# One decoder layer on one core: rare paths under one branch, one item's row products moved, tokens of the last items turned earlier

## The chip, the cores and the metric

The kernel runs on one core of a Trainium2 chip. The metric is the device time of one execution in microseconds; the program is launched once and nothing is computed on the host. The five engines of the core are TensorE (PE in the profile, with its weight loads as PEld), VectorE (DVE), ScalarE (ACT), GpSimd (POOL) and SyncE (SP). Each works through its own queue in order, and they meet through semaphores. SP issues plain DMAs; POOL issues the indirect DMAs, which gather or scatter rows by a table of indices.

## What is computed

The reference is one decoder layer over 4 sequences of 512 tokens of width 256, all in float32: a selective scan, a gated linear attention over a context, and a mixture of 8 experts of which each token takes two. After each of the three stands a residual sum and a layer norm. Only the last one matters here:

```python
# x2: the 2048 tokens after the second norm; 8 experts, w1, w3: 256 x 1024, w2: 1024 x 256
top_vals, top_idx = top_k(x2 @ gate_w, 2)          # two experts for each token, with weights m1, m2
for e in the two experts of a token:
    y += m_e * (silu(x2 @ w1[e]) * (x2 @ w3[e])) @ w2[e]
out = layernorm(x2 + y)
```

Which token goes to which expert is known only on the chip. The first two parts use a fast form that holds as long as some values stay in bounds; otherwise an exact, slow form must be computed in their place.

## The kernel before

**Stages.** `layer1` does the scan, `attend_fast` the attention, both for all four sequences; `route` then finds for each sequence the two experts of every token, and `close` writes the normed rows to DRAM: to up to three copies `xd` from which tokens are gathered, and to `yd`, in which the sums are built. `tables` turns the routing into three tables of int32 (`tok`: row to gather, `wat`: where its weight lies, `dest`: row to add to). There are four versions v of the tables: v=0 when two sequences are routed, v=1 when three are, v=2 for all four, and v=3 for overflow blocks.

**Items.** The tokens of an expert are handled in blocks of 128. An item is one block (G=1) or two (G=2). For an item:

- `fetch` (L1512) gathers the rows on POOL;
- `turn` transposes them on TensorE into `pt` (L1582), and a VectorE copy (L1586) makes `xgT`;
- `up` multiplies by w1 and w3 (L1597, tile `pu`), ScalarE takes the silu (L1602, `si`), VectorE the product (L1603, `ht`); it yields after each PSUM tile, four times for G=1 and eight for G=2;
- `down` fetches the weights of the tokens (`weigh`, L1612), multiplies by w2 (`product`, L1619, tile `po`), scales on ScalarE (L1639, `y`) and adds the rows to `yd` by an indirect DMA (`scatter`, L1625).

These are the row products: those with w2.

**Order.** `work` goes over a list of items and keeps one item `pending`: in each step it turns and does `up` of item i, and only then `down` of item i-1, so that the `ht` of an item is ready when TensorE comes to its row products. The lists are `early` (experts 0 and 1, one block each, v=0), `mid` (experts 3 to 7, v=1), `late` (v=2, and five overflow blocks), and `final` (expert 2, four single blocks). `early` has a call of `work` of its own, during which the fourth sequence is still being finished: its norm, its routing and its tables are the generator `last`. After this call the last early item is sent through `down` at once, then what is left of `last` is issued, then a second call of `work` takes `mid` and `late`. In its second step `overflow` makes the tables v=3 and the number of overflow blocks `items`.

Statements set the order of one engine only in part. A scheduler lays the instructions into the queues by its own estimates, so that instructions of `last` stand among those of the items.

**Weights.** Each expert has 3 MB (w1, w3, w2, each one DMA on SP's queue, L1494). They go into a ring of three places; the DMA of a place waits until TensorE has read what lay there.

**End.** `finale` handles the four blocks of expert 2. In its first step it does the pending `down`, then loads all of `yd` into `x1` (L1707) for the last norm, and gathers the rows of its own four blocks from `yd`. Their products are added in SBUF (`settle`, L1763), normed and scattered straight into the output (`put`). The norm of all other rows (`norm_all`: statistics L1681 and L1682, scaling on VectorE L1694 and on ScalarE L1699) is spread between the items, as one long list on VectorE's queue; its rows are stored by SP (L1710).

**Rare paths.** Two things are decided at the end by a value that every engine loads into a register (L1822, `items`; L1855, `isure`), each with a branch of its own: `tc.If(n_items > NOV0)` (L1826) for more than five overflow blocks, and `tc.If(sure == 0)` (L1859) for the exact form of the whole layer, which has the first branch in it once more. With the inputs of this case neither is taken, so both are jumped over. At the end of each the queue holds waits for all its DMAs, on POOL also an instruction that sets the semaphores of its indirect DMAs (INC_SWDGE_SEM in the profile).

Of the kernel before, what the change touches and what calls it, by code (L numbers as in the profile page):

```python
# [1 line left out]

# [7 lines left out]
F32 = mybir.dt.float32  # L10
AF = mybir.ActivationFunctionType
ALU = mybir.AluOpType
# [30 lines left out]
def decoder_kernel(ctx: ExitStack, tc: tile.TileContext, t: dict, out: bass.AP):  # L43
# [61 lines left out]
    x1 = x1T = eT = wide = val = shed = None  # L105

# [843 lines left out]
    def attend_fast(ap, hrp, np_, pt, tri, onw, mix, part, gatew, close, rt, route):  # L950
# [4 lines left out]
        with ExitStack() as hs:  # L955
# [198 lines left out]
            nc.vector.tensor_tensor(isure, top, flag, ALU.mult)  # L1154
            return tails

    def layers23(fast):
# [3 lines left out]
        NF = FF // P  # L1161
        with ExitStack() as rest:
            mp = pool(rest, "l2", 1)

            dest, tok, wat = (
                [mp.tile([P, n], I32, tag=f"{s}{v}", name=f"{s}{v}")
                 for v, n in enumerate((P, P, P, NOV))]
                for s in ("dest", "tok", "wat")
            )
            eid = mp.tile([P, NOV], I32, tag="eid", name="eid")  # L1170
            items = mp.tile([1, 1], I32, tag="items", name="items")
# [21 lines left out]
            dr = rest.enter_context(tc.tile_pool(name="dr", bufs=1, space=DRAM))  # L1193

            xds = [
                dr.tile([(v + 2) * S, D], F32, tag=f"xd{v}", name=f"xd{v}") for v in range(3)
            ]
            wds = [
                dr.tile([(v + 2) * 2 * S, 1], F32, tag=f"wd{v}", name=f"wd{v}") for v in range(3)
            ]  # L1200
            yd = dr.tile([NT, D], F32, tag="yd", name="yd")
# [236 lines left out]
            def overflow():  # L1438
# [41 lines left out]
                nc.vector.tensor_copy(items, cum[0:1, NE - 1 : NE])  # L1480


            loads = 0

            def load_expert(e):

                nonlocal loads
                ew = ring[loads % 3]
                loads += 1
                w1 = ew.tile([P, 2, FF], F32, tag="w1", name="w1")  # L1490
                w3 = ew.tile([P, 2, FF], F32, tag="w3", name="w3")
                w2 = ew.tile([P, NF, D], F32, tag="w2", name="w2")
                for w, n in ((w1, "w1"), (w3, "w3"), (w2, "w2")):
                    nc.sync.dma_start(  # L1494
                        out=w, in_=t[n][bass.ds(e, 1)].rearrange("o (k p) f -> p (o k) f", p=P)
                    )
                return w1, w3, w2

            def weights_of(e):
                if isinstance(e, int):  # L1500
                    return load_expert(e)
                i = e[0]
                return load_expert(nc.values_load(
                    eid[0:1, i : i + 1], engines=[mybir.EngineType.SP], min_val=0, max_val=NE - 1,
                    skip_runtime_bounds_check_because="it is at most NE - 1 by its minimum",
                ))

            def fetch(v, cols):

                xg = xgp.tile([P, 2, D], F32, tag="xg", name="xg")  # L1510
                for g, c in enumerate(cols):
                    nc.gpsimd.indirect_dma_start(  # L1512
                        out=xg[:, g, :], out_offset=None, in_=xds[min(v, 2)][:, :],
                        in_offset=bass.IndirectOffsetOnAxis(ap=tok[v][:, c : c + 1], axis=0),
                    )
                return xg

            def own(e, *blocks):  # L1520
                return [e * NS + j for j in blocks]

            def static(v, e, *blocks):
                return v, own(e, *blocks)

            early = [(e, [static(0, e, 0)]) for e in range(NEARLY)]
            mid = [(e, [static(1, e, 0, 1)]) for e in range(NEARLY + 1, NE)]
            mid[-1][1].append(static(2, NE - 1, 2, 3))
            late = [(e, [static(2, e, 2, 3)]) for e in range(NE - 2, NEARLY, -1)]
            late += [(e, [static(2, e, 1, 2), static(2, e, 3)]) for e in range(NEARLY)]  # L1530
            late += [((i,), [(3, [i])]) for i in range(NOV0)]

            final = (NEARLY, [static(1, NEARLY, 0), static(1, NEARLY, 1)])
            final[1].extend([static(2, NEARLY, 2), static(2, NEARLY, 3)])
            rare = [((i,), [(3, [i])]) for i in range(NOV0, NOV)]

            weights = [load_expert(0), load_expert(1)]
# [29 lines left out]
            ring.append(right)  # L1567
# [8 lines left out]
            out_t = out.rearrange("b s d -> (b s) d")  # L1576

            def turn(xg, G):
                ps = pt.tile([P, 2, TS], F32, tag="pt", name="pt3")
                for g in range(G):  # L1580
                    for k in range(2):
                        nc.tensor.transpose(  # L1582
                            ps[:, k, g * P : (g + 1) * P], xg[:, g, k * P : (k + 1) * P], ident
                        )
                xT_ = xtp.tile([P, 2, TS], F32, tag="xgT", name="xgT")
                nc.vector.tensor_copy(xT_[:, :, : G * P], ps[:, :, : G * P])  # L1586
                return xT_

            def up(xT_, G, w1, w3, ht):

                N, U = G * P, TS // (G * P)
                for f in range(0, NF, U):
                    ps = pup.tile([P, 2, U, N], F32, tag="pu", name="pu")
                    for u in range(U):
                        for j, w in enumerate((w1, w3)):
                            for k in range(2):
                                nc.tensor.matmul(  # L1597
                                    ps[:, j, u, :], w[:, k, (f + u) * P : (f + u + 1) * P],
                                    xT_[:, k, :N], start=(k == 0), stop=(k == 1),
                                )  # L1600
                    si = sip.tile([P, U * N], F32, tag="si", name="si")
                    nc.scalar.activation(si, ps[:, 0].rearrange("p u n -> p (u n)"), AF.Silu)  # L1602
                    nc.vector.tensor_tensor(  # L1603
                        ht[:, f * N : (f + U) * N], ps[:, 1].rearrange("p u n -> p (u n)"), si, ALU.mult
                    )
                    yield

            def inner(G):
                return htp.tile([P, NF * G * P], F32, tag="ht", name="ht")

            def weigh(wg, v, c):
                nc.gpsimd.indirect_dma_start(  # L1612
                    out=wg, out_offset=None, in_=wds[min(v, 2)][:, :],
                    in_offset=bass.IndirectOffsetOnAxis(ap=wat[v][:, c : c + 1], axis=0),
                )

            def product(ps, g, G, ht, w2):
                for f in range(NF):
                    nc.tensor.matmul(  # L1619
                        ps, ht[:, (f * G + g) * P : (f * G + g + 1) * P], w2[:, f, :],  # L1620
                        start=(f == 0), stop=(f == NF - 1),
                    )

            def scatter(rows, v, c, src, **kw):
                return nc.gpsimd.indirect_dma_start(  # L1625
                    out=rows[:, :],
                    out_offset=bass.IndirectOffsetOnAxis(ap=dest[v][:, c : c + 1], axis=0),
                    in_=src, in_offset=None, bounds_check=NT - 1, oob_is_err=False, **kw,
                )

            def down(v, cols, ht, w2):
                ps = pop.tile([P, 2, D], F32, tag="po", name="po")
                y = yp.tile([P, 2, D], F32, tag="y", name="y")
                wg = xgp.tile([P, 2], F32, tag="wg", name="wg")
                for g, c in enumerate(cols):
                    weigh(wg[:, g : g + 1], v, c)
                for g, c in enumerate(cols):
                    product(ps[:, g, :], g, len(cols), ht, w2)
                    nc.scalar.activation(y[:, g, :], ps[:, g, :], AF.Copy, scale=wg[:, g : g + 1])  # L1639
                    scatter(yd, v, c, y[:, g, :], compute_op=ALU.add)  # L1640

            def work(visits, weights, ahead=(), between=None):

                after = [e for e, _ in (*visits, *ahead)][len(weights) :]
                line = [(n, v, cols) for n, (_, its) in enumerate(visits) for v, cols in its]
                xgs = [fetch(v, cols) for _, v, cols in line[:2]]
                pending = None
                for i, (n, v, cols) in enumerate(line):  # L1650
                    G = len(cols)
                    xT_ = turn(xgs.pop(0), G)
                    w1, w3, w2 = weights[n]
# [312 lines left out]
```

## Time and profile before

| | us |
|---|---|
| time, median of 3 runs (lowest to highest) | 719.35 (714.34 to 723.76) |
| time of the profiled execution | 718.58 |
| its span, first to last instruction | 716.7 |
| TensorE busy | 663.3 (93%) |
| TensorE weight loads busy | 502.6 (70%) |
| VectorE, ScalarE, GpSimd busy | 307.1, 240.2, 220.4 |
| mean granted TensorE clock | 0.958 of full speed |

Times in the profile count from the first instruction. An engine's busy time leaves out register, branch, semaphore and DMA-issuing instructions; these are found by their source line, with a q behind the engine's name (POOLq). In a timeline each row has start, length, engine, line, operation, tiles, a count, and in brackets how long the engine sat idle before it and what released it. One `product` or one matmul of `up` in the source makes two TensorE records.

### The profile page before, as it was taken

The page shows a single profiled execution, that of the slowest core. Times are in us where ns is not written, and L with a number is a line of the kernel's source. Part 1 is how long each engine was busy: PE and PEld are TensorE (multiplying, and loading weights), DVE is VectorE, ACT ScalarE, POOL GpSimd, SP SyncE. Part 2 cuts the span into 40 slices and gives each one's busy share as a digit, 9 for nine tenths or more (in the row PEclk, how much of TensorE's full clock was granted, in tenths as well). Part 3 has the DMA queues.
Part 4 walks back from the last instruction along what each step waited for, and adds up shares of the span by engine and source line. Part 5 has one row for each costly group of instructions (what it writes and reads, how often), then busy time and mean ns, then how long its engine had stood idle before and what let it go on. Part 6 is the DMA issues. An engine that isn't in the chain of part 4 may idle for free. (4 is left out here: it accounts for less than half of the span.)

```text
span 716.7 us, 9223 instructions
## 1 busy us (share of the span) xinstructions
PE 663.3 (93%) x3447; PEld 502.6 (70%) x3447; DVE 307.1 (43%) x788; ACT 240.2 (34%) x460; POOL 220.4 (31%) x248
## 2 busy tenths in 40 slices
PE   5979879998999899889999999999999999999991
PEld 2413356765633445778888888888888999999890
DVE  0796855669453787856222111211111121111640
ACT  2438760223366575443212111111111111211450
POOL 0412231000144557366033332233321412332210
PEclk9999998999988899799999999999999999999996
DMA  8200050110820305695546625345661624882620
GB/s 280 100 1 0 1 176 1 30 30 9 303 70 1 118 19 176 219 321 165 188 135 206 205 62 160 112 126 177 200 193 37 185 75 140 294 294 57 206 84 16
DMA packets 61119, 92.71 MB, mean 129 GB/s; under 512 B 8728, under 2 KB 47968, under 8 KB 60800
## 3 DMA queue, kind: packets, MB, share of 16 engines
q1 hardware_dynamic: 51872, 80.25, 32.7%
q0 software_dynamic: 8096, 9.60, 7.0%
q10 hardware_dynamic: 1088, 2.10, 0.8%
q8 instruction: 31, 0.51, 0.3%
q14 instruction: 32, 0.26, 0.1%
HBM read 78.78 MB, written 13.80 MB: 129 GB/s over the span
## 5 line engine op out<-in xcount | busy, mean ns | idle before, releaser
L1597 PE MATMUL pu<-xgT,w 128*128 128x128 f32 (+1 forms) x1600 | 266.6, 327 | 1.6 <-DVE xgT L1586 1.5
L1597 PEld LDWEIGHTS pu<-xgT,w 128*128 128x128 f32 x1600 | 243.2, 193 | 23.9 <-ACT si L1602 1.9
L1603 DVE TENSOR_TENSOR ht<-pu,si 128x256 f32<-128x256 f32 x148 | 62.6, 423 | 227.5 <-ACT si L1602 227.0
L1619 PE MATMUL po<-w,ht 128*128 128x256 f32 x592 | 136.4, 380 | 2.5 <-DVE ht L1603 2.5
L1602 ACT ACTIVATE si<-pu 128x256 f32<-128x256 f32 x148 | 56.7, 384 | 196.3 <-PE pu L1597 194.7
L1619 PEld LDWEIGHTS po<-w,ht 128*128 128x128 f32 x592 | 109.0, 190 | 17.6 <-DVE ht L1603 3.3
L1625 POOL DMA_INDIRECT yd<-y,dest x33 | 53.3, 1616 | 146.6 <-ACT y L1639 127.0
L202 PE MATMUL xz<-xT,win 128*128 128x512 f32 x128 | 59.9, 624 | 10.3 <-DMA win<-in_win 7.9
L1512 POOL DMA_INDIRECT xg<-xd,tok x37 | 36.9, 997 | 80.7 <-PE pt L1582 65.6
L202 PEld LDWEIGHTS xz<-xT,win 128*128 128x128 f32 x128 | 24.7, 197 | 43.9 <-issue 38.8
L981 POOL TENSOR_TENSOR ct<-ct,tri 128x128 f32<-128x128 f32 x64 | 32.7, 529 | 47.2 <-ACT ct L980 44.6
L1639 ACT ACTIVATE y<-po,wg 128x256 f32<-128x256 f32 x33 | 15.6, 474 | 92.5 <-PE po L1619 92.5
L418 PE MATMUL fpy<-mt,xs 128*128 128x512 f32 (+3 forms) x128 | 39.5, 462 | 0.9 <-DVE fsz L422 0.8
L221 DVE SCALAR_TENSOR_TENSOR acc<-xp,convw,acc 128x2048 f32<-128x2048 f32 x12 | 30.7, 2571 | 21.6 <-POOL acc L216 21.6
L980 ACT ACTIVATE ct<-pq,eT 128x512 f32<-128x512 f32 (+3 forms) x64 | 30.6, 523 | 22.9 <-PE pq L970 22.8
L970 PE MATMUL pq<-x1T,ctxT 64*128 64x512 f32 (+3 forms) x128 | 33.8, 501 | 3.3 <-ACT ct L980 3.2
L1612 POOL DMA_INDIRECT wg<-wd,wat x33 | 32.6, 989 | 9.9 <-issue 9.6
L418 PEld LDWEIGHTS fpy<-mt,xs 128*128 128x128 f32 x128 | 23.4, 202 | 13.6 <-issue 7.2
L988 PE MATMUL ph<-ct,val 128*64 128x512 f32 (+3 forms) x128 | 32.7, 495 | 0.0
L1586 DVE COPY xgT<-pt 128x256 f32<-128x256 f32 (+1 forms) x25 | 13.8, 551 | 41.6 <-PE pt L1582 41.6
L439 PE MATMUL fpo<-fwout,fsz 128*128 128x256 f32 x128 | 29.9, 394 | 0.0
L970 PEld LDWEIGHTS pq<-x1T,ctxT 64*128 64x128 f32 x128 | 13.7, 193 | 23.0 <-ACT ct L980 10.9
(263 smaller groups left out, 623.2 us busy)
## 6 DMA issues: line engine op xcount, KB each, us to landing
w<-in_w SPq DMA_DIRECT2D x57, 1024.0 KB
xd<-x SPq DMA_DIRECT2D x9, 512.0 KB
xT<-in_xT ACTq DMA_DIRECT2D x4, 512.0 KB
ctxT<-in_ctxT SPq DMA_DIRECT2D x1, 2048.0 KB
val<-in_ctx SPq DMA_DIRECT2D x4, 512.0 KB
fxr<-in_x SPq DMA_DIRECT2D x4, 512.0 KB
yd<-x SPq DMA_DIRECT2D x4, 512.0 KB
x<-yd SPq DMA_DIRECT2D x4, 512.0 KB
```

Source lines behind the costliest of these rows:

```text
L202: nc.tensor.matmul(ps, win[:, k, c * P : (c + 1) * P], xT[:, k, b * S : (b + 1) * S], start=(k == 0), stop=(k == 1),)
L418: nc.tensor.matmul(ps[:, j * P :], xs[j][:, c, :], mt[b][j], start=(j == 0), stop=(j == NB - 1),)
L970: nc.tensor.matmul(ps[:, :w], ctxT[rows, p, s0 : s0 + P], x1T[rows, p, s0 : (b + 1) * S], start=True, stop=True,)
L981: nc.gpsimd.tensor_tensor(ct[:, :P], ct[:, :P], tri, ALU.mult)
L988: nc.tensor.matmul(po[DH * e : DH * (e + 1), tb * P :], val[:, b * NB + tb, 2 * p + e, :], cts[e], start=(tb == 0), stop=(tb == NB - 1),)
L1512: nc.gpsimd.indirect_dma_start(out=xg[:, g, :], out_offset=None, in_=xds[min(v, 2)][:, :], in_offset=bass.IndirectOffsetOnAxis(ap=tok[v][: ...
L1597: nc.tensor.matmul(ps[:, j, u, :], w[:, k, (f + u) * P : (f + u + 1) * P], xT_[:, k, :N], start=(k == 0), stop=(k == 1),)
L1602: nc.scalar.activation(si, ps[:, 0].rearrange("p u n -> p (u n)"), AF.Silu)
L1603: nc.vector.tensor_tensor(ht[:, f * N : (f + U) * N], ps[:, 1].rearrange("p u n -> p (u n)"), si, ALU.mult)
L1612: nc.gpsimd.indirect_dma_start(out=wg, out_offset=None, in_=wds[min(v, 2)][:, :], in_offset=bass.IndirectOffsetOnAxis(ap=wat[v][:, c : c + ...
L1619: nc.tensor.matmul(ps, ht[:, (f * G + g) * P : (f * G + g + 1) * P], w2[:, f, :], start=(f == 0), stop=(f == NF - 1),)
L1625: return nc.gpsimd.indirect_dma_start(out=rows[:, :], out_offset=bass.IndirectOffsetOnAxis(ap=dest[v][:, c : c + 1], axis=0), in_=src, in_ ...
```

## The change

The diff does three things, and moves the expert code into functions of its own for it.

1. **One branch at the end.** `overflow` now forms one number, `items`: 0 when nothing rare is needed, 1 when only further overflow blocks are, 2 or more when the fast form does not hold. All engines load this one number, `finale` asks for it before the last `settle`, and `tc.If(case > 0)` holds both rare paths. So that the overflow path can stand outside the pools of the common path, the tables v=2 and v=3 are stored to DRAM (`tds`), and `many` loads them again; `tok`, `wat` and `dest` of a version become three parts of one tile `tab`. The rare path for overflow blocks now also does expert 2 once more.
2. **The last early item's row products** are no longer issued before the second call of `work` but are handed to it as `pending`: they come after the first `up` of `mid`.
3. **The tokens of the last items are turned sooner:** in `finale`, item i+1 is turned after the third of the four steps of item i's `up`, not before its own.

```diff
-            weights, pending = work(early, weights, mid)
-            down(*pending)
+            weights, pending = xp.work(xp.early, weights, xp.mid)
             for _ in last:
                 pass
-            weights, pending = work(
-                mid + late, weights, [final], lambda i: overflow() if i == 1 else None
+            weights, pending = xp.work(
+                xp.mid + xp.late, weights, [xp.final], lambda i: overflow() if i == 1 else None,
+                pending,
             )
-            ys, sent = finale(final, weights[0], pending)
-            n_items = nc.values_load(items, ...)
-            with tc.If(n_items > NOV0):
...
+            return xp.finale(xp.final, weights[0], pending)
...
-        layers23(True)
-    sure = nc.values_load(isure, ...)
-    with tc.If(sure == 0):
-        kept = ExitStack()
-        with kept:
-            activations(False)
-            layer1_steps()
-            layers23(False)
+        case = layers23(True)
+    with tc.If(case > 0):
+        with tc.If(case == 1):
+            many()
+        with tc.If(case > 1):
+            kept = ExitStack()
+            with kept:
+                activations(False)
+                layer1_steps()
+                n_items = layers23(False)
+            with tc.If(n_items > NOV0):
+                many()
```

In `work`:

```diff
-            def work(visits, weights, ahead=(), between=None):
+        def work(visits, weights, ahead=(), between=None, pending=None):
...
-                pending = None
                 for i, (n, v, cols) in enumerate(line):
```

In `finale`:

```diff
+            ahead = turn(xgs.pop(0), 1)
             for i, (v, (c,)) in enumerate(line):
-                xT_ = turn(xgs.pop(0), 1)
+                xT_ = ahead
                 hts.append(inner(1))
                 for q, _ in enumerate(up(xT_, 1, w1, w3, hts[-1])):
...
+                    if q == 2 and xgs:
+                        ahead = turn(xgs.pop(0), 1)
...
             product(ps[:, 0, :], 0, 1, hts[-1], w2)
+            case = nc.values_load(items, ...)
             settle(N - 1, ps[:, 0, :])
             scales(rows[N - 1], rows[N - 1] + 1)
             put(N - 1)
-            return ys, sent
+            return case
```

In `overflow` and `attend_fast`:

```diff
-            nc.vector.tensor_tensor(isure, top, flag, ALU.mult)
+            nc.vector.tensor_tensor(sure, top, flag, ALU.mult)
...
-                nc.vector.tensor_copy(items, cum[0:1, NE - 1 : NE])
+                for td, tb in zip(tds, tabs[2:]):
+                    nc.sync.dma_start(out=td, in_=tb)
+                if not fast:
+                    nc.vector.tensor_copy(items, cum[0:1, NE - 1 : NE])
+                    return
+                more = rt("more", [1, 1])
+                nc.vector.tensor_scalar(more, cum[0:1, NE - 1 : NE], NOV0 + 0.5, None, ALU.is_gt)
+                nc.vector.scalar_tensor_tensor(more, sure, -2.0, more, ALU.mult, ALU.add)
+                nc.vector.tensor_scalar(items, more, 2.0, None, ALU.add)
```

The order in which the built program lays this into the queues is part of the change:

- TensorE, at the end of `early`: the first early item's row products are followed at once by the matmuls of the fourth sequence's routing (L1329, they read `hot`). The eight of the second early item stood between them; now two of them stand behind the turn of the first `mid` item, which follows the routing, and six behind that item's `up`. The turn of the second `mid` item stands after these six.
- POOL, before the four adds of the fourth sequence's `hv` (L1076): one weight gather fewer (L1612, tile `wgf`); it stands behind them.
- VectorE: the adding up of the fourth sequence's routing logits (L1062) stands before the statistics of `hv` (L63), no longer behind the first of them.
- SP: the store of v=2's tables stands between the weights' DMAs after the last `wd` store, that of v=3 some six weight DMAs later; the w2 that goes to the second early item's place stands behind the next expert's w1 and w3.
- SP, the store of the fourth sequence's `yd` (L1432): it waits for the scatter of the first early item, no longer for that of the second.
- All engines, at the end: one load and one branch, in the place of the first pair. On POOL the load stands behind the last scatter in both kernels.

## The prediction

> **What bounds the kernel now.** I read the page's busy times first, then the slices, the chain of waits, and the timeline at the places that the change touches.
>
> ```profile
> PE 663.3 (93%) x3447; PEld 502.6 (70%) x3447; DVE 307.1 (43%) x788; ACT 240.2 (34%) x460; POOL 220.4 (31%) x248
> PE   5979879998999899889999999999999999999991
> PEclk9999998999988899799999999999999999999996
> ```
>
> TensorE is the bound; from 340 us on it hardly stops. No part of the change removes a matmul, so only places where TensorE stands still or runs slowly can give anything. There are three near the edits: the end, where no matmul runs after 701.2 us but the span goes on to 716.7; the joint between `early` and `mid` (slices 18 and 19); and one hole in `finale`.
>
> **1. One branch.** The end of POOL's queue, asked for by source line (columns: operation, count, shortest/median/longest ns, first and last start in us):
>
> ```profile
> L1826 POOLq EVENT_SEMAPHORE  x4: 17/43/4112, 704.5 to 708.8; - x4
> L1826 POOLq COMPARE_BRANCH  x1: 53/53/53, 704.0 to 704.0; - x1
> L1826 POOLq INC_SWDGE_SEM  x1: 598/598/598, 708.9 to 708.9; - x1
> ```
>
> ```profile
> L1859 POOLq EVENT_SEMAPHORE  x6: 17/30/43, 713.0 to 713.4; - x6
> L1859 PEldq COMPARE_BRANCH  x1: 5333/5333/5333, 703.7 to 703.7; - x1
> L1859 POOLq COMPARE_BRANCH  x1: 45/45/45, 709.9 to 709.9; - x1
> L1859 POOLq INC_SWDGE_SEM  x1: 576/576/576, 713.5 to 713.5; - x1
> ```
>
> The last scatter is issued at 703.65 and lands 5.1 us later; the 4112 ns wait ends with it at 708.8. Then POOL sets the semaphores (0.6), loads the flag and branches at 709.9, is not heard of until 713.0, runs six waits and a second INC_SWDGE_SEM to 714.1, and the end of the program takes 2.6. The other engines are through at 709.5. So POOL's second pair costs 714.1 - 709.5 = **4.6 us**, of which 3.1 lie between the branch and its target.
>
> [...]
>
> In the changed kernel POOL branches once, at about 704.05, over some 750 instructions. That jump is a long one now, but lies beside the landing of the scatter. Alone it would take 3.1 and be over at 707.2. But all engines jump at about that time; the rows for such a crowd are ScalarE 3.4, VectorE 4.5, TensorE 5.3 us, so 707.4 to 709.4 against the landing at 708.8. POOL then goes on at 708.8 to 709.4 with one INC and the 2.6 of the end: gain 4.6 to 4.0, taken as **-4.3**. The load asked for earlier hides nothing more on POOL, since there it still stands behind the last scatter. Outer bounds: 1.5 (the gap is paid anyway) and 4.8.
>
> The rest of this edit: two stores of tables (192 KB and 62 KB; an issue on SP takes about 0.4 in the timeline) and two more VectorE operations on one number (0.13 us for the like, L1480). Behind the first store on SP stands a w1 that waits for TensorE anyway (issued at 339.7 in the trace, the table is ready at 331.6). The second waits for v=3's table (364.5); behind it stands a w1 whose place comes free only when the third `mid` item's `up` ends (it begins at 363.97 and by the rate before it lasts 14): 13 us of cover. Cost 0; if the cover went, each us of delay would come off a ring that is three places deep.
>
> **2. Row products behind the next loop's first item.** The joint in the timeline, TensorE's and VectorE's rows of it:
>
> ```profile
> 312.27 4.91 PE L1619 MATMUL po<-w,ht 128*128 128x256 f32 x22
> ...
> 314.33 2.79 POOL L1076 TENSOR_TENSOR hv<-hv,x 128x256 f32<-128x256 f32 x4
> ...
> 317.56 1.13 PE L1619 MATMUL po<-w,ht 128*128 128x256 f32 x4 [0.38 <-DVE ht L1603]
> ...
> 319.52 0.19 DVE L1326 TENSOR_TENSOR hot<-oh 128x32 bf16<-128x32 f32 x1
> ...
> 320.82 1.13 PE L1619 MATMUL po<-w,ht 128*128 128x256 f32 x4 [2.13 <-DVE ht L1603]
> ...
> 321.79 0.18 PE L1329 MATMUL prt<-hot,tri_b 128*128 128x40 bf16 x1
> ```
>
> TensorE waits twice for the second early item's `ht` (2.5 us), because ScalarE fits the norm's root and its table loads between the silus. Moving these products removes exactly those waits. But what is late next? In the changed queue the routing matmuls of L1329 stand right behind the first early item's products, and these end early: of the 22 records the first 14 are theirs, 14 x 0.223 = 3.1, so at 315.4. Then TensorE can only wait for `hot`. In the trace `hot` ends at 319.7, and nobody minded, since TensorE had the second item's products to do. How much earlier will it be? It hangs on the adds of `hv`, which POOL starts when its gathers are out, one each 1.25 us. One gather now stands behind them, so they run 313.1 to 315.9. From the last add to the end of `hot` the trace takes 2.6; the logits' sum moved up takes the chain no further back, as the statistics stand in between on VectorE. So `hot` is done at about 318.5, and TensorE stands still for **3.1 us in one piece, where it stood 2.5**. After it come the turn and two of the products, which cover the 0.69 of the VectorE copy; the second turn has two products (0.9) to cover its copy (0.69 and about 0.25 of hand-over): 0.1 more. The matmuls themselves are all still there.
>
> The clock goes with it:
>
> ```profile
> 321.00:322.00 1.00, 1.00 (x10) 0.81 (x11) 0.00 (x0) 1.00 (x3) 0.56 (x1) 0.97 1.07 344
> 322.00:323.00 1.00, 1.00 (x8) 1.00 (x6) 0.41 (x2) 0.98 (x3) 1.00 (x1) 0.50 0.14 44
> ```
>
> By one-us windows (the third number from the end is the granted clock) it is halved from 322.0 to 325.4, which costs half of 3.4, 1.7 us. [...] The trace shows that two holes with work between them were enough. So I charge one halved stretch before and after, difference 0; bounds -1.7 (none after) and +1.7 (two). With `hot` between 317.5 and 319.7 the wait is 0.4 less to 1.8 more than before. Together -2.1 to +3.6, taken as **+0.7**.
>
> The moved `down` issues also a weight gather, which stays ahead, and a scatter, which goes from 327 to about 344; behind it on POOL wait gathers for the fifth `mid` item, not needed for tens of us. SP's `yd` store, which waited for that scatter until 331.27, goes at about 325. The w2 for this place is issued at about 341 instead of 331.7; its products come after three more items' `up`, some 50 us on. All hidden by the depth of three.
>
> **3. Tokens turned sooner.** One hole in `finale`:
>
> ```profile
> 676.95 2.02 PE L1597 MATMUL pu<-xgT,w 128*128 128x128 f32 x16 [1.54 <-DVE xgT L1586]
> ```
>
> The copy to `xgT` runs at 676.39 though the turn is done at 674.5, since VectorE is in the long list of the norm. At the other two joints of `finale` TensorE has no hole, so nothing is to be had there. In the changed queue the copy stands five instructions further up that list (two aggregates, a statistic, an `ht`, a scaling: 1.1 us), so the matmuls can start at 675.8. But four records of row products (0.9) that filled the time between turn and copy come later now. TensorE's wait goes from 1.54 to about 1.4 and it turns without a gap later: **-0.25**; bounds -1.5 (hole gone) and +0.9 (the copy is no earlier, and the filler is lost).
>
> **Sum**: -4.3 + 0.7 - 0.25 = -3.85. Against the profiled execution's 718.58 (span 716.7) that is **714.7 us**; the median of the runs shown, 719.35, lies 0.8 above the profiled one, so 715.5 from there. 2% is about what a measurement of this kernel can tell from no change: 14 us, and the shown runs alone lie -5.0 to +4.4 around their median.
>
> **Rivals.**
> - A, *the jump is paid anyway*: with five engines fetching at once, POOL's jump ends some 3 us after the landing. For it: TensorE's 5.3. Against: that one started beside two others as well and landed with them. Gain 1.5, so 718.58 - 1.5 + 0.45 = 717.5.
> - B, *the joint closes*: `hot` early, no halved clock, the hole in `finale` gone: -4.8 - 2.1 - 1.5 = 710.2. For it: the halved stretch hung on little. Against: `hot`'s chain is serial on VectorE. With a low draw of the runs it can pass 2%.
> - C, *weights come late* (slower): the two stores and the postponed w2 on SP's queue turn the ring into one of two places. The 3 MB of an expert at the 230 GB/s of the stretch 600 to 650 take 13 us, a single block's visit 10.8; seven or eight such visits at +2.2 give +17, so 732 after the gain. It decides once the delay on SP passes the 13 us of cover above. Against: TensorE shows no wait for a weight after 340 us, and both stores have their data early.
> - D, *the change does nothing measurable*: the end has a cost that the gap only hides; 718.6.
>
> **Chances**: forecast 0.50, A 0.14, B 0.20, C 0.08, D 0.08. Forecast, A and D are within 2%; of B I give 0.14 to a gain over 2%, since its parts are at their ends and a low draw is needed, C counts as slower. The range goes from a B with a low draw to an A or D with a high one: 705.5 to 721.5; the likeliest case alone is 711.5 to 718.
>
> **What would show it.** Right: one pair of load and branch for each engine, POOL's waits ending with the last landing or within 0.6 of it, and 3.2 us from there to the span's end, where it was 7.9; TensorE waiting some 3 us for `hot` before L1329's matmuls; no wait for `ht` before the second early item's products; a wait of over 1 us for `xgT` left in `finale`. Wrong: POOL silent for 3 us after the landing; L1329 without a wait; clock 0.5 in no window of the joint, or in seven us of it; matmuls waiting for a w after 340 us.

## The result, and the profile after

The changed kernel takes **717.0 us** (median of 22 runs, 712.4 to 719.0), the kernel before in the same series 721.9 (22 runs, 712.9 to 724.1): ratio **0.9949, interval 0.9925 to 0.9972**, which is 3.7 us; the two medians lie 4.9 apart. A second series gave 0.9919, interval 0.9889 to 0.9949, or 5.9 us. So 4 to 6 us were won, in the forecast's direction and size, and less than 2% of the time.

The profiled execution of the changed kernel took 712.4 us, with a span of 710.6 where before had 716.7. Its page first: TensorE's busy share has not moved, as no matmul went.

```profile
PE 661.6 (93%) x3447; PEld 501.5 (71%) x3447; DVE 308.0 (43%) x790; ACT 240.3 (34%) x460; POOL 219.6 (31%) x248
PEclk9999998999998999899999999999999999999997
```

**The end.** The one branch asked for by its source line (columns as before: operation, count, shortest/median/longest ns, first and last start in us):

```profile
L1910 POOLq EVENT_SEMAPHORE  x6: 17/30/43, 706.9 to 707.3; - x6
...
L1910 PEldq COMPARE_BRANCH  x1: 3718/3718/3718, 698.9 to 698.9; - x1
...
L1910 POOLq COMPARE_BRANCH  x1: 53/53/53, 703.6 to 703.6; - x1
L1910 POOLq INC_SWDGE_SEM  x1: 598/598/598, 707.4 to 707.4; - x1
```

There is one pair of load and branch. POOL branches at 703.6, is heard of again at 706.9 and runs six waits of which none lasts over 43 ns: when POOL came back from its jump the last scatter had landed. From INC_SWDGE_SEM to the end of the span it is 3.2 us, as forecast. The issue of the last scatter in POOL's timeline, before and after:

```profile
703.65 0.98 POOL L1625 DMA_INDIRECT out<-ro,dest  x1 [7.53 <-DVE ro L1694]
```

```profile
703.27 0.98 POOL L1285 DMA_INDIRECT out<-ro,tab  x1 [7.63 <-DVE ro L1349]
```

From there to the end of the span it is 710.6 - 703.27 = **7.3 us; before, 716.7 - 703.65 = 13.05**. This stretch is called the tail below.

**The joint.** Timeline of all engines, TensorE's rows and the two that feed `hot`:

```profile
312.35 0.98 PE L1257 MATMUL pu<-xgT,w 128*128 128x128 f32 x4 [0.39 <-issue]
...
312.62 2.79 POOL L1099 TENSOR_TENSOR hv<-hv,x 128x256 f32<-128x256 f32 x4
...
313.77 1.03 PE L1257 MATMUL pu<-xgT,w 128*128 128x128 f32 x7 [0.45 <-issue]
...
314.64 3.19 PE L1279 MATMUL po<-w,ht 128*128 128x256 f32 x14
...
318.48 0.19 DVE L1676 TENSOR_TENSOR hot<-oh 128x32 bf16<-128x32 f32 x1
...
318.73 0.18 PE L1679 MATMUL prt<-hot,tri_b 128*128 128x40 bf16 x1 [0.90 <-DVE hot L1676]
```

`hot` is done at 318.67, where the forecast had 318.5. Two errors met in this: POOL's adds ended at 315.4, 0.5 sooner than forecast, and from there to `hot` it took 3.3 us, not 2.6. TensorE's wait for `hot` is 0.90 us and not 3.1, because TensorE comes late itself: the first early item's products begin at 314.64 and end at 317.83 (forecast: 315.4), behind an `up` with gaps that the profile calls "issue", waiting for nothing it can show.

**The last items.** VectorE's copy and the matmuls that wait for it, in the timeline:

```profile
675.14 0.42 DVE L1246 COPY xgT<-pt 128x256 f32<-128x256 f32 x1
...
675.71 1.02 PE L1257 MATMUL pu<-xgT,w 128*128 128x128 f32 x7 [1.49 <-DVE xgT L1246]
```

The hole of 1.54 us has become 1.49 here. After 340 us it is the only wait that TensorE has (the list of its waits from there on):

```profile
PE pu L1257 <- DVE xgT L1246: 1.5, 1, 1.5
```

So no weight was late, though both stores of tables and the postponed w2 stood on SP's queue.

### The profile page after: what moved, and what is told of

Same layout as the page of the kernel before. It is cut to its first block, busy times and chain, and to the rows that moved or that the text cites. A ratio compares the mean times of both kernels' runs of the same rounds, so it can differ in the third digit from the quotient of the medians.

```text
span 710.6 us, 9202 instructions
## 1 busy us (share of the span) xinstructions
PE 661.6 (93%) x3447; PEld 501.5 (71%) x3447; DVE 308.0 (43%) x790; ACT 240.3 (34%) x460; POOL 219.6 (31%) x248
## 5 line engine op out<-in xcount | busy, mean ns | idle before, releaser
L1285 POOL DMA_INDIRECT yd<-y,tab x33 | 53.3, 1615 | 147.1 <-ACT y L1299 127.9
L1213 POOL DMA_INDIRECT xg<-xd,tab x37 | 37.0, 1000 | 80.3 <-PE pt L1242 65.5
L1272 POOL DMA_INDIRECT wg<-wd,tab x33 | 32.7, 992 | 9.9 <-issue 9.6
```

Source lines behind the costliest of these rows:

```text
L1213: nc.gpsimd.indirect_dma_start(out=xg[:, g, :], out_offset=None, in_=xds[min(v, 2)][:, :], in_offset=bass.IndirectOffsetOnAxis(ap=tok[v][: ...
L1272: nc.gpsimd.indirect_dma_start(out=wg, out_offset=None, in_=wds[min(v, 2)][:, :], in_offset=bass.IndirectOffsetOnAxis(ap=wat[v][:, c : c + ...
L1285: return nc.gpsimd.indirect_dma_start(out=rows[:, :], out_offset=bass.IndirectOffsetOnAxis(ap=dest[v][:, c : c + 1], axis=0), in_=src, in_ ...
```

## One table for all ten profiles

Spans of single profiles differ by more than any part of this change. To see where, I cut each trace at the same four events: the second turn (start of VectorE's second copy to `xgT`, the second early item), the fifth turn (third item of `mid`; two expectations below call it the fifth `mid` item's), the start of the last scatter, and the end. "Halved" is the time at half clock in the joint's stretch, counted in windows of 3.41 us, the step in which the granted clock changes in these traces (last section); "rest" is the stretch less 1.71 for each, which is an estimate: half of a window in which TensorE works throughout. The stretches bear it out, with 63.8 on average at two halved windows and 60.1 at none, 1.8 for each.

```
kernel                     to turn 2  turn 2-5  halved  rest  turn 5-scatter  scatter-end
before                      302.5      60.5       1     58.8     340.7          13.05
changed                     302.0      60.6       0     60.6     340.6           7.33
single branch alone         305.7      60.1       0     60.1     340.7           7.49
moved rows alone            305.5      64.2       2     60.8     340.8          12.33
sooner tokens alone         303.4      64.2       2     60.8     340.7          12.58
short rare paths            305.4      64.0       2     60.6     340.7           7.41
changed, once more          304.4      60.7       0     60.7     340.4           7.08
late scatter                305.5      63.2       2     59.7     341.0           4.14
weights held                303.4      63.2       2     59.8     340.5           7.45
rows back, late scatter     304.3      59.0       0     59.0     341.2           4.10
```

The last column tells kernels apart by what they do; the first and the joint vary between executions by several us, in good part with the clock; the column before the last hardly varies. Each row is one profile, though: what a tail promises still has to be compared with the times of whole runs, and for the late scatter the two do not agree.

## The experiments

The first four ran together, each with one part of the change or of the cost.

### The single branch alone

The changed kernel with the other two parts undone:

```diff
             weights, pending = xp.work(xp.early, weights, xp.mid)
+            xp.down(*pending)
...
-                pending,
...
-                xT_ = ahead
+                xT_ = turn(xgs.pop(0), 1)
...
-                    if q == 2 and xgs:
-                        ahead = turn(xgs.pop(0), 1)
```

> The kernel before with the single branch alone; the row products and the turning of tokens stand where they stood. Theory (the gain of the change is POOL's second load, branch and jump): 4.3 us less than before by the prediction's sum; the two profiles suggest up to 5.7, since in the changed kernel the last scatter lands earlier as well (its waits are over 4.0 us after the issue, before they ended 5.1 after it). One pair of load and branch per engine, and about 3.2 us from POOL's INC_SWDGE_SEM to the end of the span. Rival (the joint's clock, which is not halved in the profile of the changed kernel, carries the gain): 1.5 us less at most here, and the rest only with the moved products.

Measured: 715.4 us, ratio 0.9918 (0.9889 to 0.9948), so 5.9 us less than before (3.8 to 8.0). Its branch in the profile, POOL's rows:

```profile
L1907 POOLq EVENT_SEMAPHORE  x6: 17/30/43, 710.1 to 710.6; - x6
...
L1907 POOLq COMPARE_BRANCH  x1: 53/53/53, 706.7 to 706.7; - x1
L1907 POOLq INC_SWDGE_SEM  x1: 598/598/598, 710.7 to 710.7; - x1
```

As in the changed kernel the jump (706.7 to 710.1) ends after the landing, and 7.5 us lie behind the last scatter's issue. This part alone gives the whole gain: rows and tokens add nothing that the times show. Its joint, with unmoved rows, shows neither a wait for `ht` nor a halved window.

### The moved rows alone

The kernel before, with:

```diff
-            def work(visits, weights, ahead=(), between=None):
+            def work(visits, weights, ahead=(), between=None, pending=None):
...
-                pending = None
...
             weights, pending = work(early, weights, mid)
-            down(*pending)
...
-                mid + late, weights, [final], lambda i: overflow() if i == 1 else None
+                mid + late, weights, [final], lambda i: overflow() if i == 1 else None,
+                pending,
```

> The kernel before with the moved row products alone; both branches stay. Theory (the joint trades one wait for another): within 1 us of before; the lead over the kernel before, read at the fifth mid item's turn, is between -0.7 and +1.0 us of what it is at the first early item, and TensorE waits 1 to 3 us for hot in place of 2.5 for ht. Rival (the joint closes, and the clock is no longer halved in it): 2 us less than before or better, and no one-us window below 1.00 between 310 and 330 us. The tail keeps its 13 us from the last scatter's issue to the end.

Measured: 723.3 us, ratio 1.0011 (0.9995 to 1.0026): nothing, or up to 1.9 us lost. The tail keeps its 12.3 us. The expectation about the lead failed: against before the kernel loses 3.7 us between the second and the fifth turn, and TensorE waits neither for `hot` nor for `ht`. But that is not the rows' doing, as the next run shows, whose rows are unmoved: its stretch has 64.2 us too. Both have two halved windows there.

### The tokens sooner, alone

The kernel before, with:

```diff
+                ahead = turn(xgs.pop(0), 1)
                 for i, (v, (c,)) in enumerate(line):
-                    xT_ = turn(xgs.pop(0), 1)
+                    xT_ = ahead
...
+                        if q == 2 and xgs:
+                            ahead = turn(xgs.pop(0), 1)
```

> The kernel before with the tokens turned sooner in the last four items alone. Theory: 0.25 us less, not to be told from zero in the times; in the trace the wait for xgT of the third last item is 1.4 to 1.5 us after a turn that comes earlier. Rival (the hole goes): 1.5 us less and no wait for xgT over 0.5 us.

Measured: 722.1 us, ratio 0.9996 (0.9981 to 1.0011). The wait for `xgT` is 1.56 us, just beyond the range that was expected; the hole stays. From the fifth turn to the last scatter the four kernels that have this part and an unmoved last scatter average 340.6, the four without it 340.7: some 0.1 us.

This profile, in TensorE's timeline, shows the gaps of the joint at their clearest, in code that is the same as before's up to here:

```profile
309.33 0.37 PE L1597 MATMUL pu<-xgT,w 128*128 128x128 f32 x1 [0.45 <-issue]
...
310.75 0.60 PE L1597 MATMUL pu<-xgT,w 128*128 128x128 f32 x3 [0.45 <-issue]
312.19 0.27 PE L1597 MATMUL pu<-xgT,w 128*128 128x128 f32 x1 [0.84 <-issue]
...
313.62 0.59 PE L1619 MATMUL po<-w,ht 128*128 128x256 f32 x1 [0.93 <-issue]
```

When the second early item's products are reached, at 321 and later, its `ht` is there. The 2.5 us that the moved rows were to remove exist in the one profile that was shown, and not in this one.

### Short rare paths

The kernel before, with both branches and both joins (the waits and the INC_SWDGE_SEM that follow a branch), and in each rare path only this (at most 15 instructions on an engine); the rare paths themselves are left out. The first rare path's old body is shown cut, and the second's is replaced in the same way:

```diff
             with tc.If(n_items > NOV0):
-                for i, (v, (c,)) in enumerate(final[1]):
-                    scatter(yd, v, c, ys[:, i, :])
-                _, pending = work(rare, [weights_of(e) for e, _ in rare[:2]])
...
+                stub(pt)
...
+    def stub(ps):
+        d_ = ps.tile([P, P], F32, tag="pt", name="std")
+        nc.gpsimd.memset(a_, 1.0)
+        for j in range(8):
+            nc.gpsimd.dma_start(out=..., in_=a_)
+        nc.tensor.transpose(d_, a_, ident)
+        nc.vector.tensor_copy(b_, d_)
+        nc.scalar.activation(c_, b_, AF.Copy)
+        nc.sync.dma_start(out=..., in_=c_)
```

The eight DMAs from POOL keep the join as it was: it still waits for the last scatter.

> The kernel before with both branches and both joins, but with a few instructions in each of the two rare paths (at most 15 on an engine) in place of the recomputation; the rare paths are thus left out. Theory (the gap after POOL's second branch is the jump over code that isn't there yet): the 3.1 us between that branch and the first wait behind it shrink to about 0.5 or less, TensorE's branch of 5.3 us to under 0.5 too, and the time is about 3 us below before; if the fetches of five engines also held up the landing of the last scatter, up to 4.2 below. Rival (a taken branch costs what it costs, whatever it jumps over): the 3.1 us stay, and the time is that of before.

Measured: 718.9 us, ratio 0.9923 (0.9893 to 0.9953), so 5.6 us less by the ratio (3.4 to 7.7); the medians differ by 3.6. The 15 runs spread over 10 us: the five fastest, 710.5 to 713.9, have a mean clock of 0.966 to 0.971, the other ten, from 716 on, 0.955 to 0.964. So the times are too wide to tell 3 from 5 us, and the size has to come from the profile. The last scatter and the first branch:

```profile
710.09 0.98 POOL L1637 DMA_INDIRECT out<-ro,dest  x1 [7.47 <-DVE ro L1706]
```

```profile
L1838 POOLq EVENT_SEMAPHORE  x5: 17/43/1662, 710.6 to 712.6; - x5
...
L1838 POOLq COMPARE_BRANCH  x1: 53/53/53, 710.4 to 710.4; - x1
L1838 POOLq INC_SWDGE_SEM  x1: 598/598/598, 712.7 to 712.7; - x1
```

Second branch:

```profile
L1851 POOLq EVENT_SEMAPHORE  x5: 17/43/43, 713.9 to 714.2; - x5
...
L1851 PEldq COMPARE_BRANCH  x1: 212/212/212, 708.2 to 708.2; - x1
...
L1851 POOLq COMPARE_BRANCH  x1: 45/45/45, 713.7 to 713.7; - x1
L1851 POOLq INC_SWDGE_SEM  x1: 567/567/567, 714.3 to 714.3; - x1
```

Two things are read here. First, the gap behind POOL's second branch is 0.2 us (713.7 to 713.9) where it was 3.1, and TensorE's branch takes 0.21 where it took 5.33: the time was that of jumping over the long body, and not of the branch as such. With short jumps the second pair costs 713.3 (end of the first INC) to 714.9, 1.6 us instead of 4.6. What the DMA engines carried while POOL was silent in the kernel before (window 709.5 to 713.3) points to what the jump waited for; these two lines are all there is (queue, kind, packets, MB, share of the 16 DMA engines). Packets of the kind that the profile calls instruction are called fetches here:

```profile
q14 instruction: 3, 0.02, 2.2%
q8 instruction: 1, 0.02, 2.0%
```

They are not the whole of the gap: the last of the four ends at 711.3, and POOL goes on at 713.0.

Second, the last scatter, issued at 710.09, has landed by 712.6: **2.5 us after the issue, where the three kernels with two long branches took 5.1 (before), 4.3 and 4.8**. The long wait in the latter two, of the moved rows and of the sooner tokens:

```profile
L1825 POOLq EVENT_SEMAPHORE  x4: 17/43/3293, 711.3 to 714.8; - x4
```

```profile
L1829 POOLq EVENT_SEMAPHORE  x4: 17/43/3804, 709.2 to 713.2; - x4
```

So the jumps of the engines held up the landing too. The same DMA view shows them beside the scatter, whose packets are those of q0, in the kernel before (703.6 to 709.0):

```profile
q0 software_dynamic: 48, 0.13, 11.0%
q8 instruction: 2, 0.03, 4.9%
q14 instruction: 6, 0.05, 3.5%
```

With short jumps (710.0 to 716.0) the scatter has the DMA engines to itself:

```profile
q0 software_dynamic: 48, 0.13, 6.1%
```

3.0 us of the second pair and 2.6 of the landing make the 5.6 by which this tail, 7.4, is shorter than that of before, 13.05. That the ratio of the times gives 5.6 as well is partly luck.

### The changed kernel once more

The second series ran the next four together.

> The changed kernel once more, beside the three below. Theory (the tail carries the gain: 13 us from the last scatter's issue to the end become 7.4): 5 us less than before, as the single branch alone gave 5.9 (0.9918); the joint and the last items give nothing that can be seen. In its trace the segment from the second early item's turn to the fifth mid item's is about 60 or about 64 us, as in the kernels with unmoved rows, by whether the clock is halved in the joint.

Measured: 715.8 us, ratio 0.9919 (0.9889 to 0.9949), 7.1 us behind the last scatter's issue, the joint at 60.7 without a halved window, and a wait for `hot` of 0.87 us.

### The last scatter behind the branch

In the changed kernel POOL's jump ends last: VectorE's waits begin at 706.4, POOL's at 706.9. POOL has nothing to do from its last but one scatter until the last rows come, so it can jump then:

```diff
             scales(rows[N - 1], rows[N - 1] + 1)
-            put(N - 1)
+            if fast:
+                apply(NTT + N - 1, rolast, ys[:, N - 1, :])
+            else:
+                put(N - 1)
             return case
...
+            if fast:
+                v_, (c_,) = line[-1]
+                nc.vector.tensor_copy(dlast, dest[v_][:, c_ : c_ + 1])
...
     with tc.If(case > 0):
+        nc.gpsimd.memset(dlast, NT)
...
+    ins = nc.gpsimd.indirect_dma_start(
+        out=out_t[:, :], out_offset=bass.IndirectOffsetOnAxis(ap=dlast, axis=0),
+        in_=rolast, in_offset=None, bounds_check=NT - 1, oob_is_err=False,
+    )
...
```

> The changed kernel, with the last scatter put behind the branch, so that POOL jumps while it waits for the last rows; a rare path sets the rows' addresses out of bounds. Theory (in the changed kernel POOL's jump of 3.3 to 3.4 us still ends later than the landing, which takes 2.5 where no engine fetches): from the last scatter's issue to the end 5.8 to 6.3 us in place of 7.3 to 7.5, so 1.1 to 1.6 us less than the changed kernel, 6.5 less than before. The jump of VectorE then ends last (its own branch stands behind the last scaling). Rival (the landing decides the tail, and the jump lies wholly beside it): 7.3 us stay.

Measured: 715.5 us, ratio 0.9909 (0.9878 to 0.9939). The last scatter and the branch by source line:

```profile
709.56 0.98 POOL L1930 DMA_INDIRECT out<-rolast,dlast  x1 [8.14 <-DVE rolast L1351]
```

```profile
L1918 POOLq EVENT_SEMAPHORE  x6: 17/30/43, 703.5 to 704.0; - x6
...
L1918 DVEq EVENT_SEMAPHORE  x2: 21/21/21, 712.0 to 712.1; - x2
...
L1918 POOLq COMPARE_BRANCH  x1: 53/53/53, 701.0 to 701.0; - x1
L1918 POOLq INC_SWDGE_SEM  x1: 578/578/578, 704.1 to 704.1; - x1
```

POOL is back at 704.7, five us before the last scatter goes out at 709.56. From there the span ends after **4.1 us** instead of 7.1 to 7.5. The scatter itself goes 0.5 later: 0.79 us after its rows are written, where it was 0.28. Net that is 2.7 us by the profile, more than the 1.1 to 1.6 expected: POOL's six waits and its INC (together 1.1 us) left the path along with the jump. VectorE's join, at 712.1, is now the last of the joins.

The times do not show this gain. The median is 0.3 us below that of the changed kernel beside it, the ratio 0.0010 (0.7 us), and each of the two intervals holds the other's ratio. The run below, with the late scatter too and a profiled tail of 4.1, is 1.1 us under the changed kernel. So the shorter tail is seen, but that a whole execution is 2.7 us shorter for it is not shown, and where the rest went stays open.

### The fourth expert's weights held back

```diff
             for w, n in ((w1, "w1"), (w3, "w3"), (w2, "w2")):
-                nc.sync.dma_start(
+                ins = nc.sync.dma_start(
...
+                if fast and loads == 4 and n != "w2":
+                    tc.add_manual_dep(ins.ins, o.last_up.ins.name, ...)
...
-                            nc.tensor.matmul(
+                            o.last_up = nc.tensor.matmul(
...
```

> The changed kernel, with w1 and w3 of the fourth expert held back until the second early item's matmuls against w1 and w3 are through (they were issued after the first early item's). Theory (the gaps in those matmuls, for which the profile names no cause, come from these 2 MB of transfers): no gaps named issue over 0.3 us there, the products of the first early item end near 315.4, and TensorE waits about 3 us for hot in one piece, as the prediction's sum had it; the time is that of the changed kernel within 1.5 us. Rival (the gaps have another cause): they stay, 1 to 4 us in all, and the wait for hot is under 1 us.

Measured: 716.0 us, ratio 0.9915 (0.9885 to 0.9946). The weights went out at 319.8 in this trace. TensorE's timeline:

```profile
309.24 0.39 PE L1265 MATMUL pu<-xgT,w 128*128 128x128 f32 x2 [0.68 <-issue]
310.66 1.00 PE L1265 MATMUL pu<-xgT,w 128*128 128x128 f32 x5 [1.03 <-issue]
...
320.06 3.19 PE L1287 MATMUL po<-w,ht 128*128 128x256 f32 x14
323.08 0.18 PE L1687 MATMUL prt<-hot,tri_b 128*128 128x40 bf16 x1
```

The gaps are there without those transfers, and there is no wait for `hot` at all. By windows (busy time of PE, PEld, DVE, ACT and POOL, granted clock, DMA share, GB/s) the DMA engines are all but idle while the gaps go on:

```profile
312.00:316.00 4.00, 3.11 (x12) 2.83 (x13) 0.46 (x2) 0.75 (x2) 3.69 (x6) 0.57 0.01 0
```

The theory of the gaps fell, and with a DMA share of 0.01 so does any other that rests on transfers at that time. What holds TensorE there stays open: all of the ten profiles but before's have these gaps, at the same place of the code, 1.0 to 4.5 us of them.

### Rows back in front, late scatter

The late scatter's kernel with the rows' move undone, by the first two hunks of the single branch's diff above (`down` directly after the first call of `work`, and no `pending` handed on).

> As the late scatter, but with the last early item's row products back in front of the routing: single branch, late scatter, tokens turned sooner. Theory (moving the rows is worth nothing): the same time as the late scatter with the moved rows within 1 us, 6.5 us less than before. Rival (the moved rows cost, as the run of them alone hints at with 1.0011): 0.8 us less than the late scatter with moved rows.

Measured: 714.6 us, ratio 0.9901 (0.9871 to 0.9931), the lowest of all, with a tail of 4.1 us and 59.0 in the joint. Against the late scatter with moved rows it is 0.8 us less, well inside both intervals: the runs can't tell the theory from its rival.

## Why the prediction was right, point by point

**1. One branch, -4.3: right in kind, too small.** Taking the gap behind POOL's second branch for the jump was right: of the 4.6 us of the second pair, 3.0 went when only the long jump went, and 1.6 us were left with short jumps. With the long jump came the four fetches (0.04 MB) that the DMA view shows in the silence.

The step that was mis-sized is "POOL then goes on at 708.8 to 709.4": it took the landing, 5.1 us after the issue, as a constant of the scatter. It was 2.5 with short jumps and no fetch beside it, and 4.3 to 5.1 with two rounds of long jumps. In the changed kernel the scatter's last packet ends 2.7 us after the issue, POOL's jump 3.6, and POOL's waits are through after 4.1. Counted over the profiles, two long branches have a tail of 12.65 us (mean of three) and one has 7.34 (mean of four): **-5.3**.

The fear of a crowd (5.3 us for POOL's jump too) was empty: beside the jumps of VectorE and ScalarE POOL's took 3.0 to 3.4 us in the four profiles with a single branch, and 2.6 and 2.9 where it jumps by itself, in the two with the late scatter. Nor did the jumps here cost by their length, as some rows of before suggest (instructions by the built program, time from the branch to the first wait behind it): POOL's first branch jumps over 150 in 0.5 us, VectorE's over 202 in 0.6, ScalarE's over 265 in 2.6, and POOL's second over some 560 in 3.1. SP's first branch in the same kernel, which the prediction did not look at, jumps over 227, with no other engine jumping, and takes 3.4 us:

```profile
L1826 SPq COMPARE_BRANCH  x1: 50/50/50, 689.2 to 689.2; - x1
L1826 SPq EVENT_SEMAPHORE  x9: 17/17/17, 692.6 to 693.2; - x9
```

Up to 202 instructions a jump took 0.2 to 0.6 us in these profiles, from 227 on 2.4 to 5.5, and not in the order of length: TensorE's single jump, the longest of all, took 3.4 to 3.9.

"Wrong" was marked by "POOL silent for 3 us after the landing". There is a silence, of some half us: 0.9 from the scatter's last packet to POOL's first wait, of which the packet's signal takes 0.5 if it takes what it took before (708.2 to 708.7). The extra stores cost nothing that can be seen.

**2. Moved rows, +0.7: the size is not contradicted, the way to it was wrong.** By the joint's rest, five kernels with moved rows average 60.3 us and five with unmoved rows 59.9, with up to 1.1 to either side; the times of the rows alone say +0.8 (-0.4 to +1.9). That +0.7 lies among these is luck. What failed is the step "these end early ... so at 315.4": it used the pace of the one trace, in which the second early item's matmuls run without a gap. In all others gaps come first, and they eat the wait that the change removes as well as the one that it adds: no wait for `ht` in four of the five unmoved kernels, and for `hot` 0.9, 0, 0.87, 0 and 0 in the moved ones. The clock was charged as one halved stretch on each side. Halved windows in the joint were 0, 2, 0, 2, 2 with moved rows and 1, 0, 2, 2, 0 without: the charge was right as a difference, and so "no window of the joint at 0.5", a wrong sign by the prediction's list, was a draw and not an effect.

**3. Tokens sooner, -0.25: some -0.1.** Copy at 675.14, matmuls at 675.71 where 675.8 was forecast, wait 1.49 where 1.4 was. One profile can't tell this from nothing, as the single branch alone has 1.49 too with the old order. Over all ten the wait averages 1.42 in the six kernels with this part and 1.55 in the four without it. The filler that comes later takes most of the gain back, as worked out.

**The level.** 714.7 started from a profiled execution of 718.6, and the runs of before have their median at 721.9 in the larger series: a draw 3 us low. The difference was forecast at -3.85 and came out as -3.7 and -5.9 in two series, with -4.9 between the medians of the first. So the absolute number was 2.3 us too low: 3.3 by the level, and 1.0 back by the larger difference. That -3.85 and -3.7 meet so closely is luck, since the parts as measured, -5.3, +0.4 to +0.8 and -0.1, add up to -4.6 to -5.0.

**The rivals.** A (the jump is paid anyway, 1.5 us less) falls with the tail of 7.3, which is 5.7 less. B (the joint closes) had its halved stretch gone in the profile, but the runs of the rows alone show no gain. C (weights late) falls, as TensorE waits for no weight. D is outside both intervals.

## What to carry to other kernels

The rare paths at the end of this program were not free, though they are never entered: the engine that jumps last paid for the jump over a body (3.1 us on POOL, 0.2 with a short one), and a DMA that everybody waits for was held up while the engines fetched for their jumps (it landed 4.3 to 5.1 us after its issue, 2.5 with short jumps). Two such branches cost more than one around both: a tail of 12.65 us against 7.34. Where an engine is idle ahead of its last piece of work, its branch can stand there; two profiles of it have the shorter tail, but the times have not confirmed the gain. And before pricing a stall that one trace shows, look whether other executions have it: cut several traces at the same events, and compare stretch by stretch.

## What the runs showed of the hardware

**The granted clock changed on a grid.** In all ten profiles every change of the granted clock lies on a grid of 3.413 us, whose phase differs from run to run. Cut on that grid, the sooner-tokens run shows it (columns: window, busy time of PE, PEld, DVE, ACT and POOL, granted clock, DMA share, GB/s):

```profile
305.74:309.16 3.42, 3.09 (x27) 2.74 (x25) 2.39 (x7) 1.78 (x3) 2.62 (x3) 1.00 0.37 102
309.16:312.57 3.41, 1.61 (x7) 1.19 (x8) 0.42 (x1) 0.38 (x1) 2.50 (x4) 1.00 0.73 217
312.57:315.99 3.42, 1.96 (x6) 1.00 (x4) 0.00 (x0) 0.00 (x0) 3.10 (x5) 0.51 1.03 406
315.99:319.40 3.41, 3.07 (x15) 2.95 (x15) 2.38 (x11) 0.98 (x3) 1.25 (x2) 0.50 0.13 47
319.40:322.81 3.41, 3.41 (x24) 3.22 (x24) 2.98 (x22) 3.27 (x5) 0.00 (x0) 0.99 0.27 29
```

The window from 309.16 is busy for 1.61 of 3.41 us and the next is halved; that one is busy for 1.96 and the next is halved again; the one from 315.99 is busy for 3.07, and the clock comes back. Over the ten traces, from 20 us to the last matmul: of the windows at full clock in which matmuls ran for under 45% of the time, 41 of 42 had a halved one behind them; of those between 45 and 70%, 44 of 73; of those above, 1 of 1740. What decides between 45 and 70% is not known; the window from 309.16, busy for 47%, is one of those with a halved one behind it. The stall of 2.1 us in before's joint fell into one window, 318.48 to 321.90, and left it busy for 1.29 us, 38%; the next ran at 0.51. The window of the changed kernel with the waits of 0.90 and 0.43 us, 317.76 to 321.17, was busy for 2.08 us, 61%, and the next ran at 1.00, as did those behind 29 of the 73 in that range.

The time at half clock up to the second turn came to 10 to 14 windows. It goes with part of the difference between executions of the same code: the second turn comes at 302.0 with 10 such windows and at 305.5 to 305.7 in the three profiles with 14, but at 302.5 and at 305.4 in two with 13. A line through the ten gives 0.9 us for each window.

**Where fetches fell among its packets, the last scatter was slower.** In all ten traces the packets of the last scatter begin 1.56 us after its issue. From the first to the end of the last they take 0.5 us in three kernels (short rare paths, whose view above shows no fetch beside them, and the two with the late scatter), 1.0 to 1.4 in the four with one round of long jumps beside it (1.1 in the changed kernel, where three fetches overlap them), and 2.2 to 3.0 in the three with two rounds (3.0 in before, where seven do). A jump beside the scatter did not always slow it: with the late scatter VectorE jumps from 709.0 to 712.0, and the packets, from 711.1 on, still take 0.5.
